# Attention contexts and conditional tiles moved into the products' PSUM banks at job boundaries, with earlier joins

## The chip, the cores and the metric

The kernel runs on one core of one Trainium2 chip. The metric is device time of one execution in microseconds (us); smaller is better. The time before is the median of three runs, and one more execution was profiled. PE is TensorE, DVE VectorE, ACT ScalarE, POOL GpSimd, SP the queue from which most transfers are issued.

## The reference, cut to what matters

The whole kernel is one transformer layer on 64 x 64 tokens of width 1024: a conditional product per batch row, attention, a residual, a second conditional layer with LoRA experts, and a quantised feed-forward part. The change touches only the first two:

```python
def _L0_cond_ref(x, condition, weights):          # x (64, 64, 1024)
    W = weights[condition]                        # (64, 64, 64)
    return jnp.einsum('bct,bcd->bdt', x, W)
...
qkv = x @ attn_qkvw + attn_qkvb                   # H = 1024, 32 heads of 32
scores = jnp.einsum('bhqd,bhkd->bhqk', q, k) * scale
probs = jax.nn.softmax(scores, axis=-1)
ctx = jnp.einsum('bhqk,bhkd->bhqd', probs, v)
```

## The kernel before, in words

**Blocks and phases.** `attention()` (line 185) works on 8 blocks of 512 tokens (b = 0..7). A block has four phases (c = 0..3), one for each pair of column chunks of Q and K. A phase is a list of "fills", each one product of seven in a Winograd-like scheme, and `run` (693) issues them one by one. `now` counts the planned time: 1.72 for a product of a Q or K job, 3.43 for one of a V job. A Q or K job (`rows_job`, 496) is seven products of 8 recorded matmuls each; a V job (`values_job`, 524) has seven of 16. Every phase except the last of the last block makes the next phase's Q and K (`qk_fill`); phases c = 0 and c = 3 also hold a V job behind them, so c = 1 and the next block's c = 0 begin right after a V job, and c = 2 and c = 3 right after a K job.

**Banks.** The seven products of a job use four PSUM banks, a, b, c, d, from the pool `ps_g` (line 79, four tiles of one bank). Their order is 1, 6, 7, 5, 2, 4, 3 (`Winograd`, 1115) in banks a, b, c, d, a, c, d. What reads a product out of its bank (`rest` in `job`, 456) is issued one product later, through the list `behind`. The last product (3, bank d) is read by one DVE instruction in a K job (line 494) and by three in a V job (line 544). ACT copies the first product (`psqp`, line 479), and the fifth accumulates into the same bank after that copy.

**Scores.** `scores` (558) issues 64 matmuls of 32x64 operands into the one tile of `ps_s` (line 228, the other four banks). `group` (665) plans what follows: exponents 2.7 apart (DVE `mx`, `prob`; ACT `prob`), the normalisation 8.1 later, the split into halves (`parted`, ACT, `ph`) 10.8 later, the transposing transfer on SP 1.7 after that (`turned`, `phT`), and 24.0 later the join (`joined`, ACT, `pT`); 9.4 in the last block from c = 1 on.

**Contexts and conditional tiles.** `context` (611) issues 64 matmuls of 64x32 operands; ACT copies them out in four pieces 0.86 apart and issues their four writes to DRAM on its own queue (`ctx_d`, line 637). `conditional_tile` (400) issues 4 matmuls with 512 columns, starts the load of the x tile two further on (SP, line 251), and plans two ACT copies (`yh`, 420), two transposing transfers and two POOL joins. Both were planned together by `contexts` (652), 13.7 after a phase's start and again 16.3 later, in the middle of a job, in the same `ps_s` tile as the scores. The tile of `ps_s` so passes from scores to contexts and back. In b = 0, c = 0 three conditional tiles stand alone.

**The order of the work** around the change is only the program order of each engine. The heap `due` sets it: `run` first issues everything whose planned time has come, then the product, then the reading out of the product before. Every DMA issued from SP's or ACT's queue takes the next of eight completion counters, and waits for the transfer that had the counter before it.

Of the kernel before, what the change touches and what calls it, by code (L numbers as in the profile page):

```python
# [11 lines left out]
F32 = mybir.dt.float32  # L12
# [3 lines left out]
AF = mybir.ActivationFunctionType  # L16
# [4 lines left out]
P = 128  # L21
# [70 lines left out]
def planes(x):  # L92

    return x.bitcast(I16).rearrange("p (n h) -> p h n", h=2)
# [90 lines left out]
def attention(tc, a, x_t, ctx_d, ident, dram, ps_g, KC, PB, NBLK, NCH, HPC, H, C, chores, early, op):  # L185
# [6 lines left out]
    nc = tc.nc  # L192
# [26 lines left out]
    with ExitStack() as ctx, ExitStack() as mid:  # L219
        def pool(stack, name, bufs, **kw):  # L220
            return stack.enter_context(tc.tile_pool(name=name, bufs=bufs, reuse_waits="tile", **kw))
# [2 lines left out]
        p2 = pool(ctx, "p2", 2, side="right")  # L224
        p4 = pool(ctx, "p4", 4, side="right")
        sm = pool(ctx, "sm1", 3, side="right")
        cop = pool(ctx, "co1", 4, side="right")
        ps_s = pool(ctx, "ps_s", 1, space=PSUM)
        wp = pool(mid, "wp1", 2, side="right")
        yp = pool(mid, "y1", 1, side="right")  # L230
# [101 lines left out]
        bqkv = act.tile([P, 3 * KC], F32, tag="bqkv", name="bqkv")  # L332
# [64 lines left out]

        Ys = [{} for _ in range(NBLK)]

        def conditional_tile(b, j, banks=None):  # L400

            xt, wg = x_of.pop((b, j))
            Y = Ys[b]
            if banks is None:
                banks = ps_s.tile([P, 4, 512], F32, tag="s", name=f"cond_{b}_{j}")
            ps = [banks[:, 2 + hf, :] for hf in range(2)]
            for hf in range(2):
                for r in range(2):  # L410
                    nc.tensor.matmul(  # L411
                        ps[hf][halves[r ^ hf], :], wg[halves[r], :], xt[halves[r], hf * 512:(hf + 1) * 512],
                        start=True, stop=True,
                    )
            if PB * b + j + 2 < PB * NBLK:
                load_x(*divmod(PB * b + j + 2, PB))

            def parted_y(hf):
                h = w.tile([P, 2, 512], I16, tag="yh", name=f"yh_{b}_{j}_{hf}", bufs=4)
                nc.scalar.copy(h, planes(ps[hf]))  # L420
                hs[hf] = h

            hs, hTs = {}, {}

            def turned_y(hf):
                h = hs[hf]
                hT = w.tile([P, 2, 512], I16, tag="yhT", name=f"yhT_{b}_{j}_{hf}", bufs=2)
                nc.sync.dma_start(
                    hT.rearrange("p h (k q) -> p (h k) q", q=P), h.rearrange("p h t -> p (h t)"), transpose=True
                )  # L430
                hTs[hf] = hT

            def joined_y(hf):
                key = f"B{hf + 1}{j // 2 + 1}"
                if j % 2 == 0:
                    Y[key] = quarter_of(b, key)
                src = hTs[hf].rearrange("p h (k q) -> p h k q", q=P)
                for r in range(2) if hf else (slice(0, P),):
                    q = halves[r ^ hf] if hf else r
                    q = slice((j % 2) * P + q.start, (j % 2) * P + q.stop)  # L440
                    dst = Y[key].bitcast(I16).rearrange("p k (q h) -> p h k q", h=2)[:, :, :, q]
                    nc.gpsimd.tensor_copy(dst, src[:, :, :, halves[r] if hf else r])  # L442

            for time, f, hf in (
                (1.7, parted_y, 0), (3.4, parted_y, 1), (3.5, turned_y, 0), (5.1, turned_y, 1), (8.5, joined_y, 0),
                (10.2, joined_y, 1),
            ):
                at(now + time, lambda f=f, hf=hf: f(hf))

        tile_at = {(0, 0, 0): (1, 0), (0, 1, 0): (1, 3)}  # L450
        for b in range(2, NBLK):
            tile_at.update(
                {(b - 2, 3, 0): (b, 0), (b - 2, 3, 1): (b, 1), (b - 1, 0, 0): (b, 2), (b - 1, 1, 0): (b, 3)}
# [99 lines left out]
        UNITS = ((1, 1), (0, 0), (1, 0), (0, 1))  # L553
        NU = len(UNITS)
        qk_of = {}
        heads = [slice(h * HD, (h + 1) * HD) for h in range(HPC)]
# [51 lines left out]
            nc.scalar.copy(planes(pT.rearrange("p a b q -> p (a b q)")), hT)  # L608
            return pT

        def context(b, c, pTs, banks):


            pc = banks[:, 0:2, :].rearrange("p r (n j q) -> p r n j q", n=NU, j=2)
            for n, pT in enumerate(pTs):
                m, t = UNITS[n]
                for jj in range(2):
                    for r in range(2):
                        for h in range(HPC):
                            rows = halves[(h % 2) ^ r]  # L620
                            nc.tensor.matmul(
                                pc[heads[h], r, n, jj, :],
                                vals[c // 2][rows, 2 * t + jj, m, (2 * c) % 4 + h // 2, h % 2, :],
                                pT[rows, jj, h // 2, halves[r]],
                                start=True, stop=True, tile_position=(rows.start, h * HD),
                            )

            def copied(n):
                m, t = UNITS[n]
                ch = m * NP + c  # L630

                co = cop.tile([P, 2, 2, C], F32, tag="co", name=f"co_{b}_{c}_{n}")
                nc.scalar.activation(  # L633
                    co.rearrange("p j r q -> p r j q"), pc[:, :, n, :, :], AF.Identity,
                    bias=bqkv[:, 2 * KC + ch:2 * KC + ch + 1],
                )
                nc.scalar.dma_start(ctx_d[2 * b + t][:, ch, :], co.rearrange("p j r q -> p (j r q)"))

            for n in range(NU):
                at(now + 0.86 * n, lambda n=n: copied(n))  # L640


        now = 0.0
        due, seq = [], itertools.count()
        behind = []

        def at(time, f):
            heapq.heappush(due, (time, next(seq), f))

        waiting, then = [], []  # L650

        def contexts(of, *place):

            tile_ = tile_at.pop(place, None)
            if not (tile_ or of):
                return
            banks = ps_s.tile([P, 4, 512], F32, tag="s", name="banks_" + "_".join(map(str, of or place)))
            if of:
                b, c, pTs = waiting.pop(0)
                assert (b, c) == of and len(pTs) == NU, (of, b, c, len(pTs))  # L660
                context(b, c, pTs, banks)
            if tile_:
                conditional_tile(*tile_, banks)

        def group(b, c):


            def begin():
                ps = scores(b, c)
                pTs = []  # L670
                waiting.append((b, c, pTs))
                for n in range(NU):
                    at(now + 2.7 * n, lambda n=n: first(n, ps, pTs))

            def first(n, ps, pTs):
                p = exponents(b, c, n, ps)
                at(now + 8.1, lambda: normalize(b, c, n, p))
                at(now + 10.8, lambda: second(n, p, pTs))

            def second(n, p, pTs):  # L680
                h = parted(b, c, n, p)
                at(now + 1.7, lambda: third(n, turned(b, c, n, h), pTs))

            def third(n, hT, pTs):
                at(now + (9.4 if b + 1 == NBLK and c else 24.0), lambda: fourth(n, hT, pTs))

            def fourth(n, hT, pTs):
                pTs.append(joined(b, c, n, hT))
                if (b, c) == (NBLK - 1, NP - 1) and len(pTs) == NU:
                    at(now + 6.8, lambda: contexts((b, c)))  # L690
            return begin
# [17 lines left out]
        def contexts_of(b, c):  # L709

            if b + 1 == NBLK and c >= 2:
                return [(b, c - 1)]
            return {0: [(b - 1, NP - 1) if b else None], 1: [(b, 0)], 2: [], 3: [(b, 1), (b, 2)]}[c]

        def phase(b, c, fills, length):
            at(now + 1.7, group(b, c))
            for n, of in enumerate(contexts_of(b, c)):
                at(now + 13.7 + 16.3 * n, lambda n=n, of=of: contexts(of, b, c, n))
            for n in range(2 if b > 0 else 0):
                at(now + n * length / 2 + 8.7, lambda: next(chores, None))  # L720
                if c in (0, NP - 1):
                    at(now + n * length / 2 + 15, lambda: next(chores, None))
            for f in fills:
                run(*f)
# [52 lines left out]
        for b in range(NBLK):  # L777
# [3 lines left out]
            for c in range(NP):  # L781
                fills, length = [], None
                if c + 1 < NP:
                    fills += qk_fill(b, c + 1)
                    if c == 0:
                        fills += v_fill(b, 1)
                        if b == 0:
                            for at_ in range(3, 7):
                                with_sums(fills, at_, v_raw, 1)
                        if b == 0:  # L790
                            at(now + 25, lambda: conditional_tile(1, 1))
                            at(now + 37, lambda: conditional_tile(1, 2))
                    if c + 2 == NP and b + 1 < NBLK:
# [21 lines left out]
        while due:  # L815
            now = max(now, due[0][0])
# [1343 lines left out]
```

## Time and profile before

| | |
|---|---|
| time before, median of 3 runs | 2372.41 us (2369.95 to 2374.94) |
| profiled execution, its own time | 2375.36 us |
| its span, first to last instruction | 2373.5 us |
| granted TensorE clock | 0.997 |
| attention in its steady part | about 70 to 1325 us of the span |
| DMA share of the 16 engines, 70 to 1325 us | 0.92, 225 GB/s |
| ACT busy, 70 to 1325 us | 523.86 of 1255 us |
| DVE busy, 70 to 1325 us | 641.31 of 1255 us |

An engine's busy time in a stretch says how much room it has. The table of waits says which engine stood still and for whom. A timeline lists one engine's instructions in order of time, merged where they repeat: start, length, engine, line, operation, tiles, count, and in brackets the idle time before it. The length of a group of matmuls reaches past the start of the next group, because matmuls are pipelined; what a group costs is read as the step from its start to the next group's start.

### The profile page before, as it was taken

The page shows a single profiled execution, that of the slowest core. Times are in us where ns is not written, and L with a number is a line of the kernel's source. Part 1 is how long each engine was busy: PE and PEld are TensorE (multiplying, and loading weights), DVE is VectorE, ACT ScalarE, POOL GpSimd, SP SyncE. Part 2 cuts the span into 40 slices and gives each one's busy share as a digit, 9 for nine tenths or more (in the row PEclk, how much of TensorE's full clock was granted, in tenths as well). Part 3 has the DMA queues.
Part 4 walks back from the last instruction along what each step waited for, and adds up shares of the span by engine and source line. Part 5 has one row for each costly group of instructions (what it writes and reads, how often), then busy time and mean ns, then how long its engine had stood idle before and what let it go on. Part 6 is the DMA issues. An engine that isn't in the chain of part 4 may idle for free.

```text
span 2373.5 us, 43652 instructions
## 1 busy us (share of the span) xinstructions
PE 2339.0 (99%) x17608; PEld 1724.4 (73%) x17608; DVE 1505.7 (63%) x2887; ACT 968.9 (41%) x1333; POOL 534.8 (23%) x647
## 2 busy tenths in 40 slices
PE   8999999999999999999999999999999999999997
PEld 7888888888888888888888548888645445454453
DVE  3574474474353544643634688999577878877787
ACT  1344344344353453443443523334344354444443
POOL 4221112111122223220000357888200000000001
PEclk9999999999999999999999999999999999999999
DMA  7899799899999999997976945657944445545454
GB/s 224 234 224 251 204 214 228 219 240 217 215 243 251 231 253 257 219 232 191 184 188 182 262 157 184 219 168 255 295 81 79 83 80 82 86 77 91 74 109 86
DMA packets 612116, 437.17 MB, mean 184 GB/s; under 512 B 362433, under 2 KB 524226, under 8 KB 609986
## 3 DMA queue, kind: packets, MB, share of 16 engines
q1 hardware_dynamic: 581234, 377.13, 63.4%
q0 software_dynamic: 12240, 40.38, 7.9%
q10 hardware_dynamic: 18432, 16.79, 3.2%
q8 instruction: 141, 2.31, 0.4%
q14 instruction: 69, 0.57, 0.1%
HBM read 257.24 MB, written 91.23 MB: 147 GB/s over the span
## 4 chain that ended last, share of the span: by engine, by line
PE 95%; DMA 2%; DVE 1%; ACT 1%; issue 0%; SPq 0%; POOL 0%; DVEq 0%; ACTq 0%; POOLq 0%
PE pga L1412 6%; PE psvc L530 5%; PE pskc L509 5%; PE psva L530 5%; PE psvd L530 5%; PE pskd L509 5%; PE pska L509 5%; PE psqa L509 4%; PE psqc L509 4%; PE psqd L509 4%; PE pba L1131 4%; PE pbc L1131 4%; PE pbd L1131 4%; PE pgb L1412 3%; PE pskb L509 2%; PE psqb L509 2%
## 5 line engine op out<-in xcount | busy, mean ns | idle before, releaser
L582 ACT ACTIVATE prob<-prob 128x512 f32<-128x512 f32 x128 | 80.6, 630 | 349.9 <-DVE prob L578 348.0
L608 ACT COPY pT<-phT 128x1024 int16<-128x1024 int16 x128 | 165.5, 1339 | 25.1 <-DMA phT<-ph 19.5
L1951 POOL DMA_DIRECT2D out_dram<-y x29 | 25.2, 869 | 655.2 <-DVE y L1943 655.2
L442 POOL COPY yB<-yhT 128x512 int16<-128x512 int16 (+1 forms) x84 | 76.0, 959 | 424.2 <-DMA yhT<-yh 424.0
L596 ACT COPY ph<-prob 128x1024 int16<-128x1024 int16 x128 | 133.6, 1044 | 60.6 <-DVE prob L590 40.8
L577 DVE TENSOR_REDUCE mx<-s 128x8 f32<-128x512 f32 x128 | 87.5, 683 | 67.0 <-PE s L568 67.0
L509 PE MATMUL psqa<-yB,wq 128*128 128x256 f32 x512 | 121.1, 379 | 0.5 <-ACT psqp L479 0.5
L509 PE MATMUL pska<-yB,wk 128*128 128x256 f32 x512 | 121.0, 379 | 0.0
L530 PE MATMUL psva<-wv,yB 128*128 128x256 f32 x512 | 115.8, 379 | 0.0
L1422 ACT COPY ng<-pga 128x256 f32<-128x256 f32 x125 | 46.5, 372 | 157.1 <-PE pga L1412 142.7
L1131 PE MATMUL pba<-wtA,x1T 128*128 128x512 f32 x240 | 109.0, 597 | 0.0
L1412 PE MATMUL pga<-woS,ug_T 128*128 128x256 f32 x432 | 107.3, 379 | 0.3 <-ACT ng L1422 0.3
L530 PEld LDWEIGHTS psva<-wv,yB 128*128 128x128 f32 x512 | 97.2, 190 | 14.0 <-issue 0.8
L509 PEld LDWEIGHTS psqa<-yB,wq 128*128 128x128 f32 x512 | 97.1, 190 | 14.0 <-ACT psqp L479 0.9
L509 PEld LDWEIGHTS pska<-yB,wk 128*128 128x128 f32 x512 | 97.3, 190 | 13.2
L633 ACT ACTIVATE co<-banks,bqkv 128x256 f32<-128x256 f32 x128 | 60.7, 474 | 111.8 <-PE banks L411 81.0
L590 DVE TENSOR_TENSOR prob<-prob,den 128x512 f32<-128x512 f32 x128 | 90.2, 704 | 4.4
L578 DVE TENSOR_TENSOR prob<-s,mx 128x512 f32<-128x512 f32 x128 | 88.5, 692 | 4.5
L1412 PEld LDWEIGHTS pga<-woS,ug_T 128*128 128x128 f32 x432 | 81.9, 190 | 12.2 <-issue 0.7
L544 DVE TENSOR_TENSOR vals<-psvd,psvu 64x256 f32<-64x256 f32 (+1 forms) x96 | 40.6, 422 | 77.5 <-PE psvd L530 76.6
L588 DVE TENSOR_REDUCE den<-prob 128x8 f32<-128x512 f32 x128 | 86.4, 675 | 0.0
L1578 ACT COPY x1T<-x1h 128x1024 int16<-128x1024 int16 x64 | 81.3, 1334 | 1.9 <-DMA x1h<-x_d 1.9
(318 smaller groups left out, 5404.0 us busy)
## 6 DMA issues: line engine op xcount, KB each, us to landing
wv<-v_d SPq DMA_DIRECT2D x56, 512.0 KB
wq<-q_d SPq DMA_DIRECT2D x28, 1024.0 KB
wk<-k_d SPq DMA_DIRECT2D x28, 1024.0 KB
wq<-in_qkvw_dram SPq DMA_DIRECT2D x100, 256.0 KB
wk<-in_qkvw_dram SPq DMA_DIRECT2D x100, 256.0 KB
wv<-in_qkvw_dram SPq DMA_DIRECT2D x50, 512.0 KB
x<-in_x_dram SPq DMA_DIRECT2D x32, 512.0 KB
ctx_d<-co ACTq DMA_DIRECT2D x128, 128.0 KB
```

Source lines behind the costliest of these rows:

```text
L509: nc.tensor.matmul(ps[:, 0:HB], A[:, SLOT[A_OF[i]], k, :], B[B_OF[i]][:, k, :], start=first and k == 0, stop=k == KQ - 1, skip_group_check ...
L530: nc.tensor.matmul(ps[:, j * VC:(j + 1) * VC], B[B_OF[i]][:, k, j * P:(j + 1) * P], A[:, k, :], start=first and j == 0 and k == 0, stop=k ...
L577: nc.vector.tensor_reduce(mx, ps[:, :, n, :, :], AX.X, ALU.max)
L578: nc.vector.tensor_tensor(p.rearrange("p j h k -> p h j k"), ps[:, :, n, :, :], mx.unsqueeze(3).to_broadcast([P, HPC, 2, C]), ALU.subtract,)
L582: nc.scalar.activation(p, p, AF.Exp, scale=scale)
L588: nc.vector.tensor_reduce(den, p, AX.X, ALU.add)
L590: nc.vector.tensor_tensor(p, p, den.unsqueeze(2).to_broadcast([P, n, C]), ALU.mult)
L596: nc.scalar.copy(h, planes(p.rearrange("p n k -> p (n k)")))
L608: nc.scalar.copy(planes(pT.rearrange("p a b q -> p (a b q)")), hT)
L1131: self.nc.tensor.matmul(ps, self.B[self.B_OF[i]][:, k, :], self.A[self.A_OF[i]][:, k, :], start=first and k == 0, stop=k == self.KQ - 1, s ...
L1412: nc.tensor.matmul(s[bank], B[:, k, :], A[:, k, :], start=first and k == 0, stop=k == 1, skip_group_check=True)
L1578: nc.scalar.copy(planes(x.rearrange("p k q -> p (k q)")), s.pop(("hT", n)))
```

## The change

Contexts are no longer planned 13.7 into a phase. A `section` now stands as a fill of no planned cost at a job boundary: at the start of phases c = 0, 1 and 3, and in c = 3 also between the K job and the V job. It holds a conditional tile, if there is one, the phase's scores and the contexts, in this order in c = 0 and with the contexts ahead of the scores otherwise; the second section of c = 3 has no scores. Phase c = 2, the last block's c = 2 and 3, and b = 0, c = 0 keep the old plan. The section's conditional tile and contexts take two banks each from `ps_g`, the products' pool, instead of the scores' tile. ACT's copies of conditional tiles and contexts are issued at once, each context copy now takes one bank (two units of it) instead of one unit of both banks, and the four writes follow in pairs. The pool of the copies has half as many tiles of twice the size. The join is planned 19.0 after the transposing transfer instead of 24.0.

```diff
-        cop = pool(ctx, "co1", 4, side="right")
+        cop = pool(ctx, "co1", 2, side="right")
...
-        def conditional_tile(b, j, banks=None):
+        def conditional_tile(b, j, ps=None):
             xt, wg = x_of.pop((b, j))
             Y = Ys[b]
-            if banks is None:
+            at_once = ps is not None
+            if not at_once:
                 banks = ps_s.tile([P, 4, 512], F32, tag="s", name=f"cond_{b}_{j}")
-            ps = [banks[:, 2 + hf, :] for hf in range(2)]
+                ps = [banks[:, 2 + hf, :] for hf in range(2)]
...
-                at(now + time, lambda f=f, hf=hf: f(hf))
-
-        tile_at = {(0, 0, 0): (1, 0), (0, 1, 0): (1, 3)}
+                if at_once and f is parted_y:
+                    f(hf)
+                else:
+                    at(now + time, lambda f=f, hf=hf: f(hf))
+
+        tile_at = {(0, 1, 0): (1, 3)}
...
-            def copied(n):
-                m, t = UNITS[n]
+            cos = {}
+
+            def copied(n, r):
+                m = UNITS[n][0]
                 ch = m * NP + c
-                co = cop.tile([P, 2, 2, C], F32, tag="co", name=f"co_{b}_{c}_{n}")
+                if r == 0:
+                    cos[n] = cop.tile([P, 2, 2, 2, C], F32, tag="co", name=f"co_{b}_{c}_{n}")
+                co = cos[n]
                 nc.scalar.activation(
-                    co.rearrange("p j r q -> p r j q"), pc[:, :, n, :, :], AF.Identity,
-                    bias=bqkv[:, 2 * KC + ch:2 * KC + ch + 1],
+                    co[:, :, :, r, :], pcs[r][:, n::2, :, :], AF.Identity, bias=bqkv[:, 2 * KC + ch:2 * KC + ch + 1],
                 )
-                nc.scalar.dma_start(ctx_d[2 * b + t][:, ch, :], co.rearrange("p j r q -> p (j r q)"))
-
-            for n in range(NU):
-                at(now + 0.86 * n, lambda n=n: copied(n))
+                if r == 1:
+                    for i in range(2):
+                        t = UNITS[n + 2 * i][1]
+                        nc.scalar.dma_start(
+                            ctx_d[2 * b + t][:, ch, :], co[:, i, :, :, :].rearrange("p j r q -> p (j r q)")
+                        )
+            return [lambda n=n, r=r: copied(n, r) for n in range(2) for r in range(2)]
...
+        def section(of, tile_, begin, scores_first):
+            def two(nm):
+                return [
+                    ps_g.tile([P, 512], F32, tag="g", name="_".join(map(str, (nm, r) + (of or tile_))))
+                    for r in range(2)
+                ]
+            if behind:
+                behind.pop()()
             if tile_:
-                conditional_tile(*tile_, banks)
+                conditional_tile(*tile_, two("cond"))
+            if begin and scores_first:
+                begin()
+            copies = context(*ready(of), two("pc")) if of else []
+            if begin and not scores_first:
+                begin()
+            for f in copies:
+                f()
...
-                at(now + (9.4 if b + 1 == NBLK and c else 24.0), lambda: fourth(n, hT, pTs))
+                at(now + (9.4 if b + 1 == NBLK and c else 19.0), lambda: fourth(n, hT, pTs))
...
             if b + 1 == NBLK and c >= 2:
-                return [(b, c - 1)]
+                return []
             return {0: [(b - 1, NP - 1) if b else None], 1: [(b, 0)], 2: [], 3: [(b, 1), (b, 2)]}[c]
 
         def phase(b, c, fills, length):
-            at(now + 1.7, group(b, c))
-            for n, of in enumerate(contexts_of(b, c)):
-                at(now + 13.7 + 16.3 * n, lambda n=n, of=of: contexts(of, b, c, n))
+            sections = [(of, tile_at.pop((b, c, n), None)) for n, of in enumerate(contexts_of(b, c))]
+            if b + 1 == NBLK and c >= 2:
+                at(now + 13.7, lambda: contexts((b, c - 1)))
+            if len(sections) == 2:
+                fills.insert(14, (0.0, lambda: section(*sections[1], None, False)))
+            if sections and any(sections[0]):
+                fills.insert(0, (0.0, lambda: section(*sections[0], group(b, c), c == 0)))
+            else:
+                at(now + 1.7, group(b, c))
...
+                            at(now + 13.7, lambda: conditional_tile(1, 0))
```

More of the change, by code (lines that the diff above doesn't have):

```diff
@@ L609, in joined, with context @@
             return pT
-        def context(b, c, pTs, banks):
-            pc = banks[:, 0:2, :].rearrange("p r (n j q) -> p r n j q", n=NU, j=2)
+        def context(b, c, pTs, pcs):
+            pcs = [pc.rearrange("p (n j q) -> p n j q", n=NU, j=2) for pc in pcs]
             for n, pT in enumerate(pTs):
@@ L621, in context @@
                             nc.tensor.matmul(
-                                pc[heads[h], r, n, jj, :],
+                                pcs[r][heads[h], n, jj, :],
                                 vals[c // 2][rows, 2 * t + jj, m, (2 * c) % 4 + h // 2, h % 2, :],
@@ L650, in attention, with ready, contexts @@
         waiting, then = [], []
[L652 to L661, printed above, removed]
-            if tile_:
-                conditional_tile(*tile_, banks)
+        def ready(of):
+            b, c, pTs = waiting.pop(0)
+            assert (b, c) == of and len(pTs) == NU, (of, b, c, len(pTs))
+            return b, c, pTs
+        def contexts(of):
+            banks = ps_s.tile([P, 4, 512], F32, tag="s", name="banks_" + "_".join(map(str, of)))
+            for n, f in enumerate(context(*ready(of), [banks[:, r, :] for r in range(2)])):
+                at(now + 0.86 * n, f)
+        def section(of, tile_, begin, scores_first):
[6 more added lines that the diff above has]
+                behind.pop()()
+            if tile_:
+                conditional_tile(*tile_, two("cond"))
[6 more added lines that the diff above has]
+                f()
         def group(b, c):
```

## The prediction

> **What bounds the kernel now.** I read the busy times, then the chain that ended last, then who waited for whom on PE.
>
> ```profile
> PE 2339.0 (99%) x17608; PEld 1724.4 (73%) x17608; DVE 1505.7 (63%) x2887; ACT 968.9 (41%) x1333; POOL 534.8 (23%) x647
> ...
> PE 95%; DMA 2%; DVE 1%; ACT 1%; issue 0%; SPq 0%; POOL 0%; DVEq 0%; ACTq 0%; POOLq 0%
> ```
>
> PE is 99% busy and 95% of the chain: only PE's time counts. PE's waits between 70 and 1325 us are almost nothing:
>
> ```profile
> PE pskb L509 <- DMA wk<-k_d: 1.0, 1, 1.0
> PE banks L411 <- issue: 0.9, 1, 0.9
> PE s L568 <- issue: 0.7, 2, 0.4
> PE pskc L509 <- DVE wk L284: 0.6, 1, 0.6
> PE banks L621 <- issue: 0.4, 2, 0.2
> ```
>
> So there is no stall to win beyond the 1.0 us. What the change can win is hidden inside PE's busy time, where PE goes from full 128x128 matmuls to small ones and back; what it can lose is that tight rows get waits. PE's timeline shows each kind of insertion alone (scores; contexts; conditional tile):
>
> ```profile
> 509.00 1.89 PE L509 MATMUL psqa<-yB,wq 128*128 128x256 f32 x8
> 510.82 1.59 PE L568 MATMUL s<-kT,qT 32*64 32x64 f32 x128
> 512.34 1.99 PE L509 MATMUL psqb<-T,wq 128*128 128x256 f32 x8
> 514.17 1.89 PE L509 MATMUL psqc<-T,wq 128*128 128x256 f32 x8
> ```
>
> ```profile
> 1173.92 1.89 PE L509 MATMUL pska<-yB,wk 128*128 128x256 f32 x8
> 1175.74 1.49 PE L621 MATMUL banks<-pT,vals 64*32 64x64 f32 x128
> 1177.16 1.99 PE L509 MATMUL pskb<-T,wk 128*128 128x256 f32 x8
> 1178.99 1.89 PE L509 MATMUL pskc<-T,wk 128*128 128x256 f32 x8
> ```
>
> A product's step from start to start is 1.727 us undisturbed. The one ahead of an insertion steps 1.82 (+0.09), the one behind 1.83 (+0.10); the scores step 1.52, contexts 1.42, so alone they cost 5.17 - 3.45 = 1.72 and 5.07 - 3.45 = 1.62 us.
>
> **Part 1, joining the insertions.** A conditional tile alone (psva at 96.97, psvc at 105.10, two V products of 3.453 between) costs 8.13 - 6.91 = 1.22. Contexts and conditional tile together (pska 468.33, pskc 474.42) cost 6.09 - 3.45 = 2.64, where apart they would cost 1.62 + 1.22 = 2.84. So an insertion that joins another saves 0.20, the +0.09 and the +0.10. The change joins contexts to scores in c = 0 of b = 1..7 (7 times), c = 1 of all blocks (8) and c = 3 of b = 0..6 (7): 22 x 0.20 = **4.5 us won**. Scores next to contexts never occur before; the bounds are 0 (nothing shared) and 0.20 + 0.10 (their own steps overlap as well). I take 0.20, from the nearest row, contexts next to a conditional tile. The second section of c = 3 only moves from mid-job to a boundary: 0.
>
> The Trainium skill, "TensorEngine Tiling (Array Packing)", Key Properties, says that a change of tiling mode drains the array. Scores, contexts and conditional tiles are three modes, so by the rule a joined section has four changes instead of five and saves one drain, not two edges; taking an edge of 0.10 for a drain, an estimate, that makes about 2.2 us instead of 4.5. The row of contexts with the conditional tile, also two modes, speaks for 0.20.
>
> **Part 2, the banks.** With a conditional tile, a section takes all four product banks: the tile takes b and a, free long before, and the contexts c and d. Bank d holds the job's last product, so PE now waits for DVE's reading of it. Before, the next job's fourth product asked for it, 5 us on. Behind a V job that reading is three instructions:
>
> ```profile
> 727.61 1.29 DVE L544 TENSOR_TENSOR vals<-psvd,psvu 128x256 f32<-128x256 f32 x3 [2.16 <-PE psvd L530]
> ```
>
> The next job started at 727.41, so d is free at +1.49, plus some 0.05 for the release to reach PE (the wk sum of DVE ended at 88.19, its reader pskc started at 88.24). In c = 1 PE gets to bank d after the edge (0.09), the conditional tile (1.02) and the first contexts, which go into c (0.09): +1.20. Stall 1.54 - 1.20 = 0.34, in b = 0..6: 7 x 0.34 = **2.4 us lost**. Behind it in PE's queue stand the scores and the next job, so all of it shows. In c = 0 the scores (1.52) go first and cover it. Behind a K job (c = 3) d is read by one instruction of 0.48, free at about +0.7, before +1.2: nothing, unless DVE is late by 0.5. Without a tile (b = 6 c = 3, b = 7) the contexts get b and a.
>
> The next job's first bank is the conditional tile's, released by ACT's yh copy of 1.01: tile finished at +1.1, copy at about +2.2, needed at +4.0 (c = 0, 1, 3) or +2.6 (V job behind the second section). Hidden, with 0.4 us to spare in the worst place. The third and fourth banks are the contexts': four copies of 0.47 and two issues of 0.33 end near +6, needed at +7.5 and later. Hidden.
>
> **Part 3, joins.** 128 joins stay 1.34 us each on ACT. With 24.0 no join before the last block waits for its transfer; with 9.4, in the last block, the longest wait of six is 5.8. So 19.0 has about 19.0 - 9.4 - 5.8 = 3.8 in hand: 0. They have to come earlier, since contexts are asked for 12 us sooner after the scores' phase. The contexts need the last join at 48.2 planned; it is issued at 39.6.
>
> **Part 4, queues.** On SP the x load moves 14 us ahead, and the two yh transposes with it (6.02 us of SP at 638.53, between those of ph); all four ph transposes of c = 1 now stand ahead of the wk load. Before, wk at 322.50 was issued 6 us after its job ended, behind yh's 7.12 us, and PE waited 1.0 for it. That wait can go (-1.0) or stay; I take -0.5. On POOL the tile's joins move 14 us ahead, beside the chores; their readers, DVE's sums of yB, come in c = 2 as before. ACT issues as many instructions as before, the smaller number of wider copy tiles costs nothing.
>
> **Sum.** -4.5 + 2.4 - 0.5 = -2.6 us. The profiled execution took 2375.4 and would take 2372.8; it lies 3.0 over the median of the runs, 2372.4, which makes **2370 us**.
>
> **Rivals.**
>
> *The edges and the wait come out better* (2366.5). If DVE's three readings don't hold PE, because the contexts' first part covers more, and wk's wait goes: -4.5 - 1.0 = -5.5, 2367; with some overlap of scores and contexts, 2366. For it: 0.34 is a difference of small numbers. Against: bank d is asked for 0.09 after the contexts start.
>
> *The joining saves nothing* (2374). Each kind may pay its own edges whatever its neighbour: 0 + 2.4 - 0.5 = +1.9. For it: scores and contexts use different shapes and were never neighbours. Against: the 2.64 of the joined insertion.
>
> *Slower: ACT is held by its own DMA issues.* The four ctx_d writes now stand ahead of the phase's first exponent and of the psqp copy, and the last of them takes the completion counter of the x load issued at the same boundary. ACT was held like this before:
>
> ```profile
> 748.54 0.48 ACT L633 ACTIVATE co<-banks,bqkv 128x256 f32<-128x256 f32 x1
> 751.99 0.33 ACTq L637 DMA_DIRECT2D ctx_d<-co  x1
> 752.35 1.04 ACT L596 COPY ph<-prob 128x1024 int16<-128x1024 int16 x1 [3.33 <-DMA wq<-q_d]
> ```
>
> Place: c = 0 of b = 1..6 and c = 1 of b = 0..6, 13 sections. The job's fifth product, at +11.05, needs psqp copied. The x load is issued at +1.25; after it lands ACT needs 0.36 + 0.53 + 0.35 (issue, exponent, copy). So it decides from a landing of 11.05 - 1.25 - 1.3 = 8.5 us on, and each us beyond costs 13 us. One x load before, issued at 689.77, held ACT until 698.88: 9.1 us. But it stood behind a Q load of 1.75 MB; here 0.5 MB stands ahead, and at 225 GB/s 1.25 MB less is 5.5 us. At 9.5 us it would cost 13: 2383.
>
> *Slower: PE is not fed.* A joined section issues 2 x 256 instructions in 2.9 us. The worst insertion before, the scores at 401.40, stepped 2.50 instead of 1.52. If each of 22 paid that: +21, 2391. Against: PE's waits for "issue" sum to 2.2 us in all of some 65 insertions.
>
> The page shows instruction transfers of 141 packets, 2.31 MB, 16.4 KB each. The Trainium skill, "Runtime: NRT & Kernel Launch", Instruction fetch mechanics, gives PE room for eight such blocks of 256 instructions, which would carry a section of two; no row here shows the depth.
>
> **How the numbers follow.** About 0.2% (4.7 us) is what a measurement of this kernel can tell from no change. Forecast, 2369 to 2372: 0.43. Better, about 2366.5, which is faster: 0.22. Nothing saved, 2374: 0.12. ACT held, from 2377 to 2390: 0.17. PE not fed, up to 2395: 0.06. So faster 0.22, the same 0.55, slower 0.23. The range 2365.5 to 2383 leaves out the upper half of ACT held, PE not fed and a little at the bottom.
>
> **What would show each step.** Right: PE's step from the last product of a job through contexts and scores to the next job's second product shows one +0.09 and one +0.10; contexts of c = 1 show a wait of 0.3 to 0.4 for DVE vals; no pT waits for phT before the last block; the wk wait is smaller. Wrong: PE waits named psqa for ACT psqp (ACT held), "issue" ahead of scores or contexts (not fed), psva for ACT yh (copies late), or wk and wq loads landing late.

## The result, and the profile after

The changed kernel takes **2491.94 us** (median of 4 runs, 2482.64 to 2494.01), beside 2372.28 for the kernel before: a ratio of **1.0496** (95% interval 1.0476 to 1.0517). The prediction said 2370, at most 2383. Its profiled execution took 2491.09 us (span 2489.3), 115.7 more than the profiled execution before.

The page of the kernel after, parts 1, 4 and 5: busy times, the shares of the chain, and one group of products (busy and mean ns of one, then idle time before it).

```profile
PE 2378.0 (96%) x17570; PEld 1757.5 (71%) x17608; DVE 1509.8 (61%) x2887; ACT 965.5 (39%) x1333; POOL 534.2 (21%) x647
...
PE 90%; issue 4%; DMA 3%; DVE 2%; ACT 1%; POOL 0%; SPq 0%; ACTq 0%; DVEq 0%; POOLq 0%
...
L513 PE MATMUL psqa<-yB,wq 128*128 128x256 f32 x512 | 151.8, 449 | 3.2 <-issue 2.8
```

"issue", time in which PE waits for nothing that the profile shows, went from 0% to 4% of the chain. PE is also 39 us busier with the same matmuls: the first product of a Q job, 379 ns a matmul before, takes 449. The table of PE's waits says where the issue time lies (us in total, times, longest). In its names psq, psk and psv are products of a Q, K or V job, with the bank as last letter; s are scores, pc contexts in the products' banks, banks contexts in the scores' tile:

```profile
PE s L572 <- issue: 41.6, 17, 4.8
PE pc L625 <- issue: 26.0, 8, 4.2
...
PE banks L625 <- ACT pT L612: 2.9, 1, 2.9
...
PE psqa L513 <- issue: 2.8, 1, 2.8
PE psqb L513 <- issue: 2.7, 3, 2.0
PE pc L625 <- DVE vals L548: 1.5, 7, 0.2
```

Scores, contexts and the two products behind them stand 73.1 us. Each of the 22 joined sections has one or two of these pauses. PE's timeline of the kernel after around one boundary (c = 1) shows the form that most have:

```profile
661.88 3.62 PE L534 MATMUL psvd<-wv,yB 128*128 128x256 f32 x16
665.43 1.09 PE L412 MATMUL cond<-x,wg 64*64 64x512 f32 x8
666.45 0.32 PE L625 MATMUL pc<-pT,vals 64*32 64x64 f32 x8
666.98 1.41 PE L625 MATMUL pc<-pT,vals 64*32 64x64 f32 x120 [0.21 <-DVE vals L548]
668.32 0.68 PE L572 MATMUL s<-kT,qT 32*64 32x64 f32 x36
672.76 1.65 PE L572 MATMUL s<-kT,qT 32*64 32x64 f32 x92 [3.77 <-issue]
674.35 2.94 PE L513 MATMUL psqa<-yB,wq 128*128 128x256 f32 x8
677.13 1.89 PE L513 MATMUL psqb<-T,wq 128*128 128x256 f32 x8
```

PE stands 3.77 us in the middle of the scores, after 36 of 128 matmuls whose operands all lie ready. The first product behind steps 2.78 (674.35 to 677.13) where 1.73 is undisturbed. The same stretch by windows (PE busy, PEld, DVE, ACT, POOL, then the granted clock, the DMA share, GB/s):

```profile
668.00:672.70 4.70, 0.99 (x75) 0.77 (x57) 0.00 (x0) 2.06 (x5) 0.00 (x0) 1.00 1.04 222
672.70:676.00 3.30, 3.23 (x96) 2.85 (x96) 1.51 (x3) 0.09 (x1) 1.64 (x2) 0.53 1.04 297
676.00:680.00 4.00, 4.00 (x19) 3.47 (x19) 1.59 (x3) 1.44 (x3) 3.09 (x7) 0.96 0.02 2
```

Behind the stall the granted clock is half for 3.4 us. In attention there are 21 such places, of 3.4, 6.8 or once 10.2 us, 99.0 us together; before there is none. The account: 73 us of stalls, up to 49 of half clock (PE at half of its rate for 99 us; in some places the half clock begins before PE goes on), 3 for contexts that wait for the readings of bank d, less some 4 that joining saves: 121 by these bounds, against 115.6 by which the first product behind attention starts later (1436.10 for 1320.48).

**What PE waits for.** The page lists 141 transfers of instructions of 16.4 KB. I set their times beside the running count of PE's recorded instructions: matmuls, weight loads and those of its sequencer, mostly waits for semaphores (449 in the kernel after; without them the remainder drifts). All 24 pauses of over 1 us between 100 and 1436 us of the kernel after begin when the count is a multiple of 256 and 193 more, and end 1.2 to 1.7 us behind the end of a transfer of instructions:

```
kernel   PE stops at   count mod 256   pause us   from the transfer's end to PE's next
after    485.9         193             4.12       1.54
after    668.8         193             3.99       1.48
after    908.5         193             4.00       1.28
after    1150.1        193             2.08       1.35
before   195.6         193             1.52       1.50
```

So a transfer brings 256 instructions and PE has run out of them. In slow stretches most of the same transfers start at counts of 256 k - 104 to 256 k - 60, so up to some 290 instructions (193 + 100) lie ready then. In a dense stretch PE runs about 180 instructions a microsecond (256 in the contexts' step of 1.42 us) and eats them before the block is there: in the stall shown, the transfer starts 1.56 us after PE has stopped (670.34 for 668.78). The kernel before shows the same limit, once, for 1.5 us, in the middle of a conditional tile behind contexts:

```profile
193.70 1.49 PE L621 MATMUL banks<-pT,vals 64*32 64x64 f32 x128
195.12 1.08 PE L411 MATMUL banks<-x,wg 64*64 64x512 f32 x4
197.13 1.08 PE L411 MATMUL banks<-x,wg 64*64 64x512 f32 x4 [0.93 <-issue]
```

### The profile page after: what moved, and what is told of

Read it like the earlier page. It is cut to its first block, busy times and chain, and to the rows that moved or that the text cites. A ratio compares the mean times of both kernels' runs of the same rounds, so it can differ in the third digit from the quotient of the medians.

```text
span 2489.3 us, 43718 instructions
## 1 busy us (share of the span) xinstructions
PE 2378.0 (96%) x17570; PEld 1757.5 (71%) x17608; DVE 1509.8 (61%) x2887; ACT 965.5 (39%) x1333; POOL 534.2 (21%) x647
## 4 chain that ended last, share of the span: by engine, by line
PE 90%; issue 4%; DMA 3%; DVE 2%; ACT 1%; POOL 0%; SPq 0%; ACTq 0%; DVEq 0%; POOLq 0%
PE psqa L513 6%; PE pga L1445 5%; PE psva L534 5%; PE psvd L534 4%; PE psvc L534 4%; PE pskc L513 4%; PE psqc L513 4%; PE psqd L513 4%; PE pska L513 4%; PE pskd L513 4%; PE pbc L1164 4%; PE pbd L1164 4%; PE pba L1164 4%; PE pgb L1445 3%; PE psqb L513 2%
## 5 line engine op out<-in xcount | busy, mean ns | idle before, releaser
L513 PE MATMUL psqa<-yB,wq 128*128 128x256 f32 x512 | 151.8, 449 | 3.2 <-issue 2.8
L513 PEld LDWEIGHTS psqa<-yB,wq 128*128 128x128 f32 x512 | 113.2, 226 | 24.9 <-issue 3.7
L572 PE MATMUL s<-kT,qT 32*64 32x64 f32 x4096 | 59.8, 246 | 41.6 <-issue 41.6
L421 ACT COPY yh<-cond 128x1024 int16<-128x1024 int16 x56 | 54.0, 1015 | 116.5 <-PE cond L412 116.5
L572 PEld LDWEIGHTS s<-kT,qT 32*64 32x64 f32 x4096 | 52.6, 141 | 54.3 <-issue 52.3
```

Source lines behind the costliest of these rows:

```text
L513: nc.tensor.matmul(ps[:, 0:HB], A[:, SLOT[A_OF[i]], k, :], B[B_OF[i]][:, k, :], start=first and k == 0, stop=k == KQ - 1, skip_group_check ...
L572: nc.tensor.matmul(ps[halves[r], h ^ r, n, jj, :], q[heads[h], m, t0:t0 + C], k[heads[h], m, t0:t0 + C], start=True, stop=True, tile_posit ...
```

## The experiments

The theories that the expectations name: **FEED**: a section of 2 x 256 small instructions (or two sections too near each other) uses up the instructions that lie ready, PE stands until the next block comes, and its clock is halved behind it. **SHAPE**: what costs is that scores and contexts, unlike small shapes, stand next to each other. **ACT**: the contexts' copies and psqp are held on ACT's queue by its own DMA issues, and through the banks PE is. **BOUNDARY** and **PLACE**: the section's place at a job's boundary costs, through banks, copies and readings, whatever its length. Below, "ratio" is to the kernel before on the same chip, with its 95% interval.

### Scores taken out of the section, 1.7 and 6.8 us behind it

```diff
-                fills.insert(0, (0.0, lambda: section(*sections[0], group(b, c), c == 0)))
+                fills.insert(0, (0.0, lambda: section(*sections[0], None, False)))
+                at(now + 1.7, group(b, c))
```

This is gap1. gap4 has `6.8 if b + 1 < NBLK else 1.7` for 1.7, and its joins 16.0 behind the transposes instead of 19.0.

> The changed kernel, but the scores of a joined phase come one product (1.73 us, 8 matmuls) behind the section instead of inside it. FEED theory (PE runs out of instructions: two sets of 256 instructions in 2.9 us are more than what lies ready, and the next block takes some 4 us to come): 1.73 us of the stall are covered, some 1.5 us stay in most of 22 places and the clock falls less often, so 2395 to 2430 us. SHAPE theory (the array stalls where 64x32 contexts and 32x64 scores meet): they no longer meet, no stall, 2373 to 2378 us. ACT theory (ACT's copies and DMA issues hold PE at the boundary): the section still stands there with all its ACT work, so it stays near 2490 us.

> The changed kernel, but the scores of blocks 0 to 6 come four products (6.9 us) behind the section, those of the last block one product; joins 16.0 instead of 19.0 behind their transposes so that they are in time. FEED theory: 6.9 us cover the coming of a block, so no stall in 20 of 22 places: before (2372) + 3 us for the wait for bank d in c = 1 + up to 5 for the last block = 2374 to 2380 us; nothing is won, as nothing is joined. SHAPE theory: the same, 2374 to 2376. ACT theory: near 2490 us.

gap1: **2440.21** us, ratio 1.0292 (1.0266 to 1.0319). gap4: **2410.06**, 1.0172 (1.0151 to 1.0192). The waits of gap1:

```profile
PE s L572 <- issue: 35.5, 20, 3.2
...
PE psqb L513 <- issue: 3.8, 1, 3.8
```

One product between the two sections (1.7 us) leaves most of the stalls, only shorter; the half clock falls to 37.5 us. With four products between them (gap4) 16.8 us of issue and 17.1 of half clock are left. The direction is FEED's, but both times are over its ranges, so FEED alone, with a distance of 7 us, is not enough. gap4's table of waits shows what else is there: psqc waits 7.6 us in four places for ACT's copies, as the ACT rival says. ACT's timeline of gap4 in one of them (ACTq is ACT's queue issuing a DMA):

```profile
747.89 1.93 ACT L421 COPY yh<-cond 128x1024 int16<-128x1024 int16 x2 [2.33 <-PE cond L412]
749.70 0.85 ACT L639 ACTIVATE co<-pc,bqkv 128x256 f32<-128x256 f32 x2
753.31 3.13 ACTq L645 DMA_DIRECT2D ctx_d<-co  x2
756.54 0.84 ACT L639 ACTIVATE co<-pc,bqkv 128x256 f32<-128x256 f32 x2 [5.99 <-DMA wv<-v_d]
```

The second two copies, which free the contexts' banks, stand 5.99 us behind two writes that wait for a weight load's landing. A second execution of gap4's kernel (the run labelled gap4_last) was taken to see how much of its waits repeats:

> The kernel of the run gap4 again, for one more profile on the chip on which the two runs with later writes are made; nothing is changed. FEED expects its waits again: six to eight stalls put down to issue (about 15 us in all), and ACT (the copies that free the contexts' banks stand behind writes that wait for a load) four waits of psqc for the copies, about 7 us in all; 2407 to 2415 us.

2408.6 us; 18 us of waits by issue, and two waits of psqc for the copies (6.1 us) in place of four.

### Few instructions, the same sections

```diff
+            for r in range(2):
+                for h in range(HPC):
+                    rows = halves[(h % 2) ^ r]
+                    nc.tensor.matmul(
+                        pcs[r][heads[h], :],
+                        vals[c // 2][rows, h, 0, (2 * c) % 4 + h // 2, h % 2, :],
+                        pTs[h].rearrange("p a b q -> p (a b q)")[rows, :],
+                        start=True, stop=True, tile_position=(rows.start, h * HD),
+                    )
...
-            for n, pT in enumerate(pTs):
-                m, t = UNITS[n]
...
```

Eight products of 512 columns stand for the 64 of 64 columns; the contexts that they make are not the right ones.

> The changed kernel with each context's 64 matmuls of 64 columns replaced by 8 of 512 columns in the same tile shapes, banks and places: the same columns stream, with an eighth of the instructions; the contexts computed are not the right ones. FEED theory: a joined section then has 16 + 32 + 256 recorded instructions instead of 528, no stall or short ones: 2350 to 2365 us, and within 4 us of its control wide_before (-4.5 for joining, +3 for bank d). SHAPE theory: the same shapes meet in the same places, so the stalls stay: 2460 to 2480 us. ACT theory: the copies and issues are the same, 2460 to 2480 us.

> Control: the kernel before with the same replacement of the contexts' matmuls (8 of 512 columns instead of 64 of 64; not the right contexts). All theories: 32 contexts of some 0.9 to 1.1 us instead of 1.42, so 10 to 16 us faster than before: 2356 to 2363 us.

wide_after (the changed kernel with it): **2372.04** us, ratio 1.0003 (0.9989 to 1.0017). wide_before (the kernel before with it): **2358.17**, 0.9944 (0.9924 to 0.9964). The waits of wide_after:

```profile
PE s L572 <- issue: 3.1, 1, 3.1
...
PE psqa L513 <- ACT psqp L483: 2.1, 4, 1.2
PE psqb L513 <- issue: 2.0, 1, 2.0
```

and wide_before's only wait by issue:

```profile
PE s L568 <- issue: 0.9, 3, 0.4
```

The sections are joined as before, the shapes meet as before, ACT's copies and writes are the same, only TensorE's instructions are fewer. Of the 120 us that the change costs, 14 are left beside the control (2372.04 - 2358.17), and the stalls are gone (6.9 us by issue in scores and products, one half-clock place of 3.4). That refutes SHAPE and ACT as the main cause. The range for wide_after was too low: FEED alone would leave nothing of the 14. The waits that the control lacks are 6 us of issue, 3.5 of ACT's copies and 2.0 of a DVE sum (psku); with 1.7 for the half clock they make 13.

### The same limit in the kernel before

If FEED is right, the kernel before must show it when nothing but the length of an insertion in mid-job is changed.

```diff
-            for n, (m, t) in enumerate(UNITS):
+            for n, (m, t) in [*enumerate(UNITS)] * 2:
```

This is double, 512 instructions an insertion. quarter has `[*enumerate(UNITS)] + [(0, UNITS[0])]` there: 320.

> Which part it changes: the kernel before, with the 64 products of each of the 32 blocks of scores issued twice into the same places (512 instructions of TensorE in one insertion, loads of weights counted, in place of 256); nothing else moves. FEED (a section of more than some 290 instructions starves TensorE of instructions, and its clock is halved for some 3.4 us after the stall): each of the 32 insertions costs its own 1.43 us, a stall of 2 to 4 us and the slower clock behind about half the stalls; 2372 + 32 x 1.43 = 2418 without stalls, so 2480 to 2580, with 20 or more waits of scores or of the product behind them put down to issue. BOUNDARY (the rival: it is the place at a job's boundary, where banks of two jobs meet, and not the number of instructions): 2410 to 2425, with no such waits.

> Which part it changes: the kernel before, with one of the scores' four units issued twice into the same place, so that each of the 32 insertions has 320 instructions of TensorE (256 in before, 512 in the run double); nothing else moves. The added work by itself is 32 x 0.36 = 11.5 us: 2384 without stalls. FEED with some 290 instructions ready when a block is asked for: only those insertions stall in which the block's edge falls near the section's first 30 to 60 instructions, 5 to 12 of 32, for 1 to 3 us each and some half clock behind: 2395 to 2425, with 8 to 30 us of waits put down to issue. If the depth were as large as a section of two (512), 2382 to 2387 and no such waits; if any doubling of a place costs, as much a matmul as in double (204 us for 512 - 256), a quarter of it: 2423.

double: **2575.84** us, ratio 1.0863 (1.0813 to 1.0913). quarter: **2414.22**, 1.0179 (1.0141 to 1.0216). The main wait of double:

```profile
PE s L568 <- issue: 92.7, 33, 6.2
```

It is the changed kernel's picture without a boundary, a bank or a second shape: 33 waits for 32 insertions, and 28 places at half clock (136.5 us). quarter stalls in 5 of its 32 insertions, and the others step 1.86 to 2.02. PE's timeline of quarter in a stalled one:

```profile
570.30 1.89 PE L509 MATMUL psqa<-yB,wq 128*128 128x256 f32 x8
572.12 1.90 PE L568 MATMUL s<-kT,qT 32*64 32x64 f32 x157
578.19 0.33 PE L568 MATMUL s<-kT,qT 32*64 32x64 f32 x3 [4.17 <-issue]
578.45 3.48 PE L509 MATMUL psqb<-T,wq 128*128 128x256 f32 x8
```

PE ran out 6 instructions (3 matmuls with their loads) short of the end of 320, waited 4.17 us, and the next product ran at half clock (3.27 in place of 1.73). An insertion of 320 stalls only where the block's edge falls badly: the five begin at counts of 256 k + 136 to 165, and none of the other 27 begins there. One of 512 stalls nearly always. The sum of quarter: added work 32 x (1.86 - 1.52) = 10.9, waits by issue of scores and of two products 15.2 + 2.5 + 2.8 = 20.5, half clock 20.5 / 2 = 10.2: 41.6, beside 45.5 measured.

### ACT's writes behind the copies

```diff
-                if r == 1:
-                    for i in range(2):
...
+            def written(n):
+                ch = UNITS[n][0] * NP + c
+                for i in range(2):
...
+            return [lambda n=n, r=r: copied(n, r) for n in range(2) for r in range(2)] + [
+                lambda n=n: written(n) for n in range(2)
+            ]
```

> Which part it changes: in the kernel of the run gap4, the four writes of a block of contexts (ctx_d) are issued behind all four copies from the contexts' banks; there, two stand behind the first two copies. The computation stays whole. ACT (a write that waits for the counter of a load's landing holds the two copies behind it, and with them the banks of the next job): the four waits of psqc for the copies (7.6 us in all in gap4) go, with the half clock behind one or two of them, and no others come: 2398 to 2405, 5 to 12 us under gap4. FEED alone: those waits are a by-product, other waits take their place, and the time stays within 3 us of gap4's 2410; the stalls put down to issue (about 15 us) stay in both.

> Which part it changes: in the kernel of the run wide_after (8 products of 512 columns stand for the 64 of the contexts, whose values are not the contexts), the four writes of a block of contexts are issued behind all four copies from the banks. ACT: the waits of psqa for psqp (2.1 us) and of psqc for co (1.9 us) go in the main, and the time falls by 3 to 6 us from wide_after's 2372 to 2366 to 2369; the rest of the 14 us to wide_before's 2358 is issue (6.9 us of waits and 3.4 us at half clock) and stays. FEED alone: 2370 to 2373.

gap4_writes is gap4 with it, wide_writes is wide_after with it.

gap4_writes: **2408.07** us, 1.0158 (1.0136 to 1.0181). wide_writes: **2372.09**, 0.9997 (0.9985 to 1.0009). In gap4 the waits of psqc for the copies are gone and the time is the same within the interval. In wide_writes psqa now waits 6.1 us for psqp, which stands behind the writes instead. So ACT's queue is held by its own DMA issues, as the rival said, but moving the writes moves the wait to another reader and wins nothing.

### Joins alone

```diff
-                at(now + (9.4 if b + 1 == NBLK and c else 24.0), lambda: fourth(n, hT, pTs))
+                at(now + (9.4 if b + 1 == NBLK and c else 19.0), lambda: fourth(n, hT, pTs))
```

> Which part it changes: in the kernel before, the joining copies come 19.0 us behind their transposes in place of 24.0; nothing else is changed. All theories: nothing, as the transposes land in time (2370 to 2374; ratio within 0.2% of 1). If a joining copy waits for a transpose with SyncE's queue held up, ACT stands for up to 3 us a time and the time rises to 2376 or more.

**2375.79** us, 1.0012 (1.0002 to 1.0023): nothing that matters here, perhaps 3 us lost.

### The scores 12 us behind the boundary

As gap4, with 11.9 for 6.8 and joins at 9.4 for 16.0.

> Which part it changes: the kernel of the run gap4 with the scores 11.9 us of product time behind the boundary's section in place of 6.8 (block 7 stays at 1.7), and, so that the weights are there for the next contexts, the joining copies 9.4 us behind their transposes in place of 16.0. So the banks and the place of contexts and conditional tiles are those of the changed kernel, but two sections lie about as far apart as in the kernel before (12 us). FEED: the stalls put down to issue fall from gap4's 16 us to 3 to 8, with no half clock or one place of it; what is left is the wait for the readings of bank d (2.8 us) and the copies that hold banks: 2378 to 2392. ACT or the place itself (rival: the boundary costs by its banks, wherever the scores are): 2400 to 2412 as in gap4. If the joining copies at 9.4 now wait for their transposes, a wait of contexts for pT shows it with its own price, and is to be taken off.

**2406.20** us, 1.0149 (1.0116 to 1.0183): outside FEED's range and inside PLACE's. Up to the first product behind attention it takes 31 us more than before; by kinds, each wait counted with what waits, products have 13.4 more and contexts 18.3. The waits of its attention are 13.5 us by issue in 13 places, 3.8 for co, 2.6 for vals, 4.0 for yh and 3.1 for pT, and there are 6.8 us at half clock. PE's timeline of gap7 shows one large stall:

```profile
460.30 1.09 PE L412 MATMUL cond<-x,wg 64*64 64x512 f32 x8
461.32 0.32 PE L625 MATMUL pc<-pT,vals 64*32 64x64 f32 x8
461.85 1.36 PE L625 MATMUL pc<-pT,vals 64*32 64x64 f32 x115 [0.21 <-DVE vals L548]
467.19 0.43 PE L625 MATMUL pc<-pT,vals 64*32 64x64 f32 x5 [3.98 <-issue]
```

Conditional tile and contexts (272 instructions) run out near their own end, with no other section near.

### The whole change without scores and contexts in one section

```diff
-            if sections and any(sections[0]):
-                fills.insert(0, (0.0, lambda: section(*sections[0], group(b, c), c == 0)))
-            else:
-                at(now + 1.7, group(b, c))
+            if sections and sections[0][0]:
+                fills.insert(7, (0.0, lambda: section(sections[0][0], None, None, False)))
+            if sections and sections[0][1]:
+                fills.insert(0, (0.0, lambda: section(None, sections[0][1], None, False)))
+            at(now + 1.7, group(b, c))
```

> Which part it changes: in the changed kernel nothing stands in one section any more: at a job's boundary the conditional tile stands alone, the scores stand one product behind it (1.7) as in the kernel before, and the contexts stand alone at the next boundary, 12 us later, which is nearly where the kernel before has them (13.7). Kept are the products' banks at the boundaries, the merged copies and the joining copies at 19.0. So it is the change without any joining of sections. FEED (length and nearness of sections are the whole loss): no stalls put down to issue beyond the kernel before's (2 us in attention), and 2370 to 2380. PLACE (the boundary's banks cost the 14 us of wide_after, or gap7's 35, by themselves): 2384 to 2406, with waits of products for the contexts' copies and of contexts for vals.

One kind of joined section stays, other than expected: in six places the second section of c = 3 still holds a conditional tile and contexts, 272 instructions, between the K and the V job.

**2377.70** us, ratio 1.0027 (1.0012 to 1.0042): FEED's range, not PLACE's. The wait of banks that the kernel before lacks:

```profile
PE pska L513 <- DVE qT L498: 4.7, 6, 1.6
```

No half clock, and no issue wait over 0.3 us; the six sections of 272 step 2.43 to 2.52, without a wait. With the products' banks, the merged copies, the earlier joins and a place at the boundary all kept, the 114 us between this kernel and the changed one (2491.94 - 2377.70) come with joining scores to contexts and with their nearness. What is left, 7 us, has one new wait of its own: the K job behind the contexts waits 4.7 us for the reading of the Q job's last bank (qT).

## Why the prediction was wrong

- **The step that failed** is the rival "PE is not fed": "A joined section issues 2 x 256 instructions in 2.9 us", priced with the worst insertion before at 1.0 us (+21, 2391) and given 0.06; the sum of the forecast (-4.5 + 2.4 - 0.5) has it at nothing. The rival's mechanism was the right one, its price was a fifth of what it is: 2 to 5 us of stall a section and a clock at half for 3.4 to 6.8 us behind, together 119.7 / 22 = 5.4 us. Its argument "PE's waits for 'issue' sum to 2.2 us in all of some 65 insertions" was a sum over insertions of 256 and 272, which the up to 290 ready instructions carry nearly always; it says nothing of 528. quarter shows how near the edge was: 320 already stalls in 5 of 32.
- The prediction said "no row here shows the depth". It could be had from the trace of before: the times of its instruction transfers against PE's running count give the limit of 256 k + 193 (at 195.6 us), and the starts from 256 k - 104 on the depth. The Trainium skill, "Runtime: NRT & Kernel Launch", Instruction fetch mechanics, from which I took room for eight blocks, also calls the crossing of a block mostly hidden. Here PE stops at most some 290 instructions behind the place where a transfer starts, and the crossing costs 2 to 5 us in a dense stretch; the measurement decides.
- The halved clock was in no step at all. The Trainium skill, "TensorE: Matmul & The Clock Gate", Part 1, says that the clock drops to half after an idle window of about 3.4 us and comes back after a busy one. The lengths of the pieces at 0.5, 3.4 and 6.8 us, agree with it. The idle time does not: 12 of the 21 pieces follow pauses shorter than 3.4 us, down to 1.99 (549.92, half from 553.4 on), and the pause of 2.08 at 1150.11 brings none; the measurement decides.
- **Part 1** (0.20 a joined section) is seen where PE is still fed. PE's timeline of the kernel after, in a c = 0 section:

```profile
603.89 3.62 PE L534 MATMUL psvd<-wv,yB 128*128 128x256 f32 x16
607.44 1.09 PE L412 MATMUL cond<-x,wg 64*64 64x512 f32 x8
608.46 1.59 PE L572 MATMUL s<-kT,qT 32*64 32x64 f32 x128
609.98 0.42 PE L625 MATMUL pc<-pT,vals 64*32 64x64 f32 x22
```

  The product ahead of the section steps 3.55 (3.45 and the edge of 0.10), the conditional tile 1.02 and the scores 1.52, as they do alone, with no edge between them. So the joining saved its edges; beside 120 us the time cannot show 4.5 (22 x 0.20 is 4.4, which moves nothing).
- **Part 2**: contexts of c = 1 wait for the readings of bank d (DVE vals), 0.21 each in the table, and step 0.53 + 1.34 = 1.87 in place of 1.42: 0.45 x 7 = 3.2, where the sum had 0.34 x 7 = 2.4. The mechanism was right. That the contexts' banks are released in time ("Hidden") holds in the changed kernel, where no product waits for them; gap4 shows psqc waiting up to 3.7 us for copies held behind writes.
- **Part 3**: within 0.2% as said (joins19), with a small loss rather than 0.
- **Part 4**: PE waits 0.7 us for wk instead of 1.0, where the sum had 0.5 less: right in direction, and of no weight.
- **ACT held by its own DMA issues** (2383): its sign, psqa waiting for psqp, is 0.5 us in the changed kernel, as before. In gap4 and wide_writes it is real as a wait, and worth a few us at most; taking it away in gap4 changed nothing.

Left open: what makes gap7 28 us slower than banks. 13 us of it are waits by issue, which banks hardly has, and 3 the half clock; the waits for ACT and DVE sum to 13.5 in gap7 and 6.7 in banks; the earlier joins (9.4) were changed with the distance, and were not tried apart. A gap7 with the conditional tile taken out of the section was written to ask this; it deadlocks and has no time. Why a section of 272 sometimes runs dry by itself is settled in part by the count at which it begins: the stalled ones of gap7 (460.30), gap4 (456.95 and 1023.12) and the kernel before (193.70) begin at 256 k + 179 to 186, so the limit of 193 falls in their last few instructions. But other sections that begin there pass (gap7, 1022.31), and why is open. The DMA engines are full in the stall shown (share 1.04), so a transfer of instructions may be late there; no run varied the load.

## What to carry to other kernels

Count TensorE's instructions, weight loads too, in each stretch of small matmuls, and compare them with what lies ready: here 256 in 1.4 us go by unseen, 272 and 320 stall now and then, and 512 cost 5 us a time. Packing small work together saves tenths of a microsecond at its edges; spreading it among large matmuls lets the next block of instructions arrive. When PE waits for "issue", set the instruction transfers against the count of executed instructions before looking for a semaphore.

## What the runs showed of the hardware

- PE stops at one fixed place, 256 k + 193 of its recorded instructions (matmuls, weight loads and its sequencer's), in all 24 pauses over 1 us of the kernel after between 100 and 1436 us, in all 32 of double, all 20 of gap1 and 6 of 7 of quarter up to the first product behind attention, and once in the kernel before; it goes on 1.2 to 1.7 us behind the end of the transfer of the next 16.4 KB, which itself takes about 1 us.
- The clock adds to a stall's price, up to 49 us to 73 in the kernel after: the stall of 3.77 us that ends at 672.76 is followed by a granted clock of 0.53 over the next 3.3 us. Not every pause is: in gap4 three of the five of over 3 us are, and the two others are waits for ACT's copies (2.94 and 3.70 us idle).
- Fewer and wider products are worth something by themselves: in wide_before the contexts' steps sum to 32.1 us in attention in place of 43.5, which is most of the 14 us by which it is faster.
